# A two-layer graph network on one core: both layer norms of a node computed early, the residual product in a loop of its own

## The chip, the cores and the metric

The kernel runs on one core of a Trainium2 chip. The metric is the time of one execution on the device, in microseconds (us). Three runs of the kernel before took 3151.96, 3153.39 and 3156.57 us, median 3153.39.

## The reference

6250 nodes with 256 features (x), 100,000 edges (src, dst). Every step is added to x:

```python
x = x + _L0_gnn_ref(_layernorm(x), W1, W2, b, src, dst)            # layer 0, graph
x = x + _L0_ffn_ref(_layernorm(x)[None], wr, br, w1, b1, w2, b2)   # layer 0, top-k ffn
x = x + _L1_gnn_ref(_layernorm(x), edges, W, att_src, att_dst, bias, W_res, ...)
x = x + _L1_ffn_ref(_layernorm(x)[None], Wr, br, W1, ..., Wo, bo)  # 8 experts
...
# _L0_ffn_ref
weights = x @ wr + br
sel_idx = top_k(weights, k)[:kk]          # half of the nodes
y = (gelu(x[sel_idx] @ w1 + b1) @ w2 + b2) * weights[sel_idx]
return zeros.at[sel_idx].set(y) + x
...
# _L1_gnn_ref
xn = layer_norm(x, ln1_g, ln1_b)
h = xn @ W                                # 8 heads of 32
e = leaky_relu(a_src[src] + a_dst[dst])   # a_src, a_dst from h
alpha = softmax of e over the edges of each dst (self loops added)
out = segment_sum(h[src] * alpha, dst) + xn @ W_res + bias
out = layer_norm(out, ln2_g, ln2_b)
return out + gelu_tanh(out @ ffn_w1 + ffn_b1) @ ffn_w2 + ffn_b2
```

So layer 1 needs, for each node, x after the layer 0 ffn, and that one depends on whether the node is among the selected half: X + wts * Y for a selected node and X for another, with Y the ffn's output.

## The kernel before

X stays in SBUF as 50 tiles of 125 nodes (NT = 50, NP = 125, D = 256, KD = 2 halves of 128 features). The stages, in order:

- **Start** (to about 165 us of the span). Edges are placed in 17 slots of 128 per tile (SL), layer 0's rows are normalized and stored to gtab in DRAM.
- **First pass** (to 1200). For each tile, POOL gathers 16 to 17 blocks of 128 rows of gtab (L209), TensorE sums them into the tile's nodes with one-hot matrices (L454), and layer 0's graph step follows. `weave` (L1207) strings the tiles' edges (L439) together with the ffn of earlier tiles, in chunks of four tiles (CHUNKS0; the last are of 3, 2 and 1). `weigh0` (L487) normalizes X for the ffn: statistics and root on DVE, z on ACT (L500), X + z written back to X, the selection weight wts on DVE, transposes of z (L506). `ffn0` (L510) is the ffn for all nodes; its output y is stored to ytab in DRAM. The framework's planner orders the engines here: it takes work by its costs and readiness, and may start later code early.
- **Select** (1200–1236). `select` finds the mask of the chosen half, a chain on DVE; wm = wts * mask (L636). The ffn of the last two chunks is traced after it.
- **Nodes' loop of layer 1** (1236–1358). Y is loaded from ytab in ten sets of five tiles, in turn on SP's and ACT's queue (L652). `mix` (L661) works on spans of 1, 2, 2 and then 5 tiles: X += wm * Y (L666), bn_stats and aggregate, one root for the span (`rs`, L182–188). `front` (L673): z on ACT (L676), two transposes (L680), two gains on ACT (L682). Then per tile the product with W and the attention columns, ph (L704, 272 wide), and the one with W_res, pr (L706, 256 wide); ACT evicts h to ht (L707), DVE the attention columns to ASAD (L708) and pr + bias to rr (L709). h goes to htab, rr to rtab. The extremes of the source terms are kept per span. The planner orders all of it.
- **Extremes and branch** (1358–1368). The extremes are reduced over the partitions (L725–733); f1I (L739) says whether the general softmax is needed; all engines load it (L751) and branch (L752). With these inputs the branch isn't taken.
- **Second pass** (1368 to the end). DVE makes the terms adsh of the destinations (L762–770). Per tile there are three groups of six blocks (s counts groups; NG = 3, GS = 6, the last block of a tile being its own rows). `fetch(s)` gathers the rows of htab on POOL into one of four ring buffers and loads own rows on SP; `fetch_tile` loads the one-hot source rows ohT (L812) and rr on SP, `onehot_t` (L819) turns them into one-hot matrices on DVE; `spread` (L827) multiplies them with adsh. Scores, exponentials, sums (L902), layer 1's ffn and the experts follow, woven. Order on PE, DVE and ACT is written by hand (`manual_schedule`, L780), that of POOL and SP is the planner's. POOL also adds the layer's constant to X (`add_o`, L967–969); the planner had 13 of the L968 operations run in the nodes' loop.

Before the second pass starts its rhythm it fetches group 0, the tile's one-hot rows and groups 1 and 2.

Of the kernel before, what the change touches and what calls it, by code (L numbers as in the profile page):

```python
# [18 lines left out]
P = 128  # L19
# [41 lines left out]
def gnn_ffn(ctx, tc, A, out):  # L61
# [114 lines left out]
    def rs(pool, dst, src, mul, add, op0=ALU.mult, name="rs"):  # L176

        p, n = src.shape[0], src.shape[-1]
        v = pool.tile([p, n], F32, name=name + "v")
        y = pool.tile([p, n], F32, name=name + "y")  # L180
        h = pool.tile([p, n], F32, name=name + "h")
# [19 lines left out]
    wm = stat.tile([NP, NT], F32, name="wm")  # L201
    sdT = edge.tile([P, 2, NT, SL], I32, name="sdT")
# [213 lines left out]
    with ExitStack() as p1:  # L416
        wp = p1.enter_context(tc.tile_pool(name="w1", bufs=1))
# [5 lines left out]
        f_w1 = load_w(wp, A["L0_ffn_w1"], "f_w1")  # L423
        f_w2 = load_w(wp, A["L0_ffn_w2"], "f_w2")
        f_b2 = bcast_load(wp, A["L0_ffn_b2"], D, "f_b2")
        f_b1 = load_cols(wp, psum, A["L0_ffn_b1"], "f_b1")
        wrs = bcast_load(wp, A["L0_ffn_wr"], D, "wrs")
        f_br = bcast_load(wp, A["L0_ffn_br"], 1, "f_br")
# [58 lines left out]
        def weigh0(t0, c):  # L487

            xT = pool.tile([P, KD, CT * NP], F32, name="xT")
            made[t0] = xT  # L490
            for j in range(c):
                t = t0 + j
                mv = pool.tile([NP, 2], F32, name="mv")
                bn(pool, mv, X[:, t, :])
                r1 = pool.tile([NP, 3], F32, name="r1")
                rs(pool, r1[:, 0:1], mv[:, 1:2], 1.0, 1e-5)
                nc.vector.scalar_tensor_tensor(r1[:, 1:2], mv[:, 0:1], -1.0, r1[:, 0:1], op0=ALU.mult, op1=ALU.mult)
                nc.vector.tensor_scalar_add(r1[:, 2:3], r1[:, 0:1], 1.0)
                z = pool.tile([NP, D], F32, name="z")
                nc.scalar.activation(z, X[:, t, :], AF.Identity, bias=r1[:, 1:2], scale=r1[:, 0:1])  # L500
                nc.scalar.activation(X[:, t, :], X[:, t, :], AF.Identity, bias=r1[:, 1:2], scale=r1[:, 2:3])
                jk = pool.tile([NP, D], BF16, name="jk2")
                nc.vector.scalar_tensor_tensor(jk, z, 1.0, f_wr, op0=ALU.mult, op1=ALU.mult, accum_out=wts[:, t:t + 1])
                pt = psum.tile([P, KD, NP], F32, name="mi")
# [3 lines left out]
                yield  # L508

        def ffn0(t0, c):  # L510
# [3 lines left out]
            for f in range(NF):  # L514
# [3 lines left out]
                h = pool.tile([P, CT * NP], F32, name="hT", bufs=NF + 1)  # L518
# [3 lines left out]
            for j in range(c):  # L522
                y = pool.tile([NP, 1, D], F32, name="y")
# [4 lines left out]
                ndma(y, ytab, t0 + j, False)  # L528
                yield


        ready = p1.enter_context(ExitStack())
        tmp = ready.enter_context(tc.tile_pool(name="ready", bufs=1))
        far = tmp.tile([1, NT, HEADS], BF16, name="far")
# [29 lines left out]
        def prepare():  # L564
            nc.gpsimd.memset(adsh, 0.0)
            nc.gpsimd.memset(far, FAR)
# [59 lines left out]
        for _ in firsts[-1][1][0]:  # L626
            pass
        for _ in weigh0(*CHUNKS0[-1]):
            pass
        nc.vector.tensor_scalar(wts, wts, f_br[0:NP, :], None, op0=ALU.add)  # L630


        ready.close()
# [993 lines left out]
```

## Time and profile before

| | us |
|---|---|
| median of 3 runs | 3153.39 (3151.96 to 3156.57) |
| the profiled execution | 3153.0 |
| its span | 3151.2 |
| PE, DVE, ACT, POOL busy | 2782.3 (88%), 2019.5 (64%), 1197.9 (38%), 1967.4 (62%) |
| L209 gathers, first pass | 800, mean 0.949 |
| L209 gathers, second pass | 850, mean 1.199 |
| mean granted TensorE clock | 0.946 |

PE is TensorE's matmuls, PEld its weight loads, DVE VectorE, ACT ScalarE, POOL GpSimd, SP the engine that only issues DMAs. Times are from the start of the span. The time of a run is 1.8 us more than the span of the profiled execution. "[5.40 <-DVEq L752]" behind an instruction says that its engine was idle 5.40 us before it, and what it waited for. Busy time of an instruction overlaps that of the next on the same engine, so that starts show the rate better than durations.

### The profile page before, as it was taken

The page shows a single profiled execution, that of the slowest core. Times are in us where ns is not written, and L with a number is a line of the kernel's source. Part 1 is how long each engine was busy: PE and PEld are TensorE (multiplying, and loading weights), DVE is VectorE, ACT ScalarE, POOL GpSimd, SP SyncE. Part 2 cuts the span into 40 slices and gives each one's busy share as a digit, 9 for nine tenths or more (in the row PEclk, how much of TensorE's full clock was granted, in tenths as well). Part 3 has the DMA queues.
Part 4 walks back from the last instruction along what each step waited for, and adds up shares of the span by engine and source line. Part 5 has one row for each costly group of instructions (what it writes and reads, how often), then busy time and mean ns, then how long its engine had stood idle before and what let it go on. Part 6 is the DMA issues. An engine that isn't in the chain of part 4 may idle for free.

```text
span 3151.2 us, 40450 instructions
## 1 busy us (share of the span) xinstructions
PE 2782.3 (88%) x12748; PEld 1979.3 (63%) x12748; DVE 2019.5 (64%) x5683; ACT 1197.9 (38%) x2215; POOL 1967.4 (62%) x1752
## 2 busy tenths in 40 slices
PE   4358889888898896947899999999999999999999
PEld 4345666666666675736776666666666666666665
DVE  7734444444444447857888787777777778787731
ACT  3302222122222222625455455354554545445332
POOL 4677777777777760257777666666666666666400
PEclk8779999999999997968999999999999999999999
DMA  5443343333333335356655545555455454544412
GB/s 124 101 149 103 111 115 112 112 112 111 112 112 112 112 103 127 103 156 177 185 163 148 168 128 149 145 140 157 129 157 146 136 160 126 162 139 137 127 50 60
DMA packets 262780, 407.55 MB, mean 129 GB/s; under 512 B 55283, under 2 KB 202207, under 8 KB 262514
## 3 DMA queue, kind: packets, MB, share of 16 engines
q0 software_dynamic: 80000, 221.18, 25.7%
q1 hardware_dynamic: 169466, 170.78, 18.4%
q10 hardware_dynamic: 13080, 12.80, 1.6%
q8 instruction: 106, 1.74, 0.2%
q14 instruction: 128, 1.05, 0.1%
HBM read 371.33 MB, written 34.04 MB: 129 GB/s over the span
## 4 chain that ended last, share of the span: by engine, by line
PE 45%; DVE 6%; ACT 3%; issue 1%; DMA 1%; POOL 0%; DVEq 0%; ACTq 0%; POOLq 0%
PE ph L1073 19%; PE py L1091 9%; PE iotaP L902 5%; PE py L986 5%; PE ph L975 4%; DVE hrow L892 1%; PE mi L948 1%; DVE lo L882 1%; PE mi L1013 1%; DMA hrow<-htab,sdT 1%; ACT L977 1%; PE pa L827 1%; DVE oh L914 1%; ACT hi L912 1%; ACT hT L977 0%
## 5 line engine op out<-in xcount | busy, mean ns | idle before, releaser
L209 POOL DMA_INDIRECT hrow<-htab,sdT x850 | 1019.3, 1199 | 501.0 <-issue 212.9
L209 POOL DMA_INDIRECT rows<-gtab,sdT x800 | 759.3, 949 | 243.6 <-issue 133.3
L1074 ACT ACTIVATE h<-ph,bi,sc 128x500 f32<-128x500 f32 (+3 forms) x448 | 321.4, 722 | 537.9 <-PE ph L1073 537.6
L454 PE MATMUL ps<-rows,oh 128*125 128x257 f32 x1600 | 434.1, 416 | 60.6 <-DMA rows<-gtab,sdT 50.3
L454 PEld LDWEIGHTS ps<-rows,oh 128*125 128x125 f32 x1600 | 313.7, 204 | 173.5 <-DMA rows<-gtab,sdT 78.5
L1073 PE MATMUL ph<-h,W 128*128 128x500 f32 (+3 forms) x896 | 371.8, 548 | 0.0
L1091 PE MATMUL py<-Wo,h 128*125 128x256 f32 x1600 | 369.3, 380 | 0.4 <-ACT h L1074 0.4
L1073 PE MATMUL ph<-wcat,W 128*128 128x500 f32 (+3 forms) x896 | 365.6, 547 | 2.3 <-ACT h L1074 2.2
L1091 PEld LDWEIGHTS py<-Wo,h 128*125 128x125 f32 x1600 | 296.3, 188 | 71.8 <-issue 28.3
L892 DVE TENSOR_TENSOR hrow<-hrow 128x768 f32<-128x768 f32 x300 | 280.5, 975 | 73.8 <-ACT hrow L877 73.8
L1094 DVE SCALAR_TENSOR_TENSOR X<-py,gate,X 125x256 f32<-125x256 f32 x400 | 173.5, 478 | 202.8 <-PE py L1091 202.6
L882 DVE SCALAR_TENSOR_TENSOR lo<-hrow,hi 128x792 fp32r<-128x792 f32 (+1 forms) x300 | 287.0, 998 | 0.0
L912 ACT ACTIVATE hi<-hrow 128x792 fp32r<-128x792 f32 (+1 forms) x300 | 236.8, 823 | 124.5 <-DVE hrow L892 124.3
L902 PE MATMUL iotaP<-hi,oh 128*125 128x264 f32 x850 | 252.2, 329 | 0.0
L1073 PEld LDWEIGHTS ph<-wcat,W 128*128 128x128 f32 x896 | 162.4, 194 | 140.9 <-issue 109.8
L1073 PEld LDWEIGHTS ph<-h,W 128*128 128x128 f32 x896 | 159.6, 194 | 106.3 <-issue 95.8
L902 PE MATMUL iotaP<-lo,oh 128*125 128x264 f32 x850 | 219.9, 291 | 4.8 <-DVE lo L882 4.7
L517 PE MATMUL ph<-xT,f_w 128*128 128x500 f32 (+3 forms) x448 | 190.2, 550 | 0.5 <-ACT xT L507 0.5
L975 PE MATMUL ph<-xT,h_w 128*128 128x500 f32 (+3 forms) x448 | 185.1, 554 | 5.1 <-ACT hT L977 4.0
L526 PE MATMUL py<-f_w,hT 128*125 128x256 f32 x800 | 182.8, 381 | 1.2 <-DVE y L527 0.4
L986 PE MATMUL py<-h_w,hT 128*125 128x256 f32 x800 | 177.6, 380 | 0.0
L902 PEld LDWEIGHTS iotaP<-lo,oh 128*125 128x125 f32 x850 | 162.7, 191 | 20.6 <-issue 8.3
(331 smaller groups left out, 3874.5 us busy)
## 6 DMA issues: line engine op xcount, KB each, us to landing
W<-in_L_ffn_W SPq DMA_DIRECT2D x224, 256.0 KB
Wo<-in_L_ffn_Wo SPq DMA_DIRECT2D x112, 256.0 KB
ohT<-dltab SPq DMA_DIRECT2D x50, 535.5 KB
hrow<-htab,sdT POOLq DMA_INDIRECT x850, 3.3
rows<-gtab,sdT POOLq DMA_INDIRECT x800, 2.8
hrow<-htab SPq DMA_DIRECT2D x50, 115.5 KB
X<-in_x ACTq DMA_DIRECT2D x10, 560.0 KB
ytab<-y SPq DMA_DIRECT2D x50, 112.0 KB
```

Source lines behind the costliest of these rows:

```text
L209: nc.gpsimd.indirect_dma_start(out=dst, out_offset=None, in_=tab, in_offset=bass.IndirectOffsetOnAxis(ap=idx, axis=0))
L454: nc.tensor.matmul(ps, oh[:, i, :], edge_rows[i], start=(s0 + i == 0), stop=(s0 + i == SL - 1))
L517: nc.tensor.matmul(ph[:, 0:n], f_w1[:, k, f * P:(f + 1) * P], xT[:, k, 0:n], start=(k == 0), stop=(k == KD - 1))
L882: nc.vector.scalar_tensor_tensor(L["lo"][:, c], L["rows"][:, c], 1.0, L["hi"][:, c].bitcast(F32), op0=ALU.mult, op1=ALU.subtract)
L892: nc.vector.tensor_tensor(h4, h4, rows[:, c, D:, None].to_broadcast([P, GS // 2, HEADS, HD]), ALU.mult)
L902: nc.tensor.matmul(tiles[t]["ps"], L["oh"][:, i, :], r[:, i, :], start=(g + i + q == 0), stop=(g * GS + i == SL - 1 and q == 1))
L912: nc.scalar.activation(L["hi"][:, c], L["rows"][:, c], AF.Copy)
L975: nc.tensor.matmul(ph[:, 0:n], h_w1[:, k, f * P:(f + 1) * P], C["xT"][:, k, 0:n], start=(k == 0), stop=(k == KD - 1))
L986: nc.tensor.matmul(py[:, i, :], C["hT"][f][:, j * NP:(j + 1) * NP], h_w2[:, f, :], start=(f == 0), stop=(f == NF - 1))
L1073: nc.tensor.matmul(ph[:, 0:n], w[:, k, f * P:(f + 1) * P], rhs[:, k, 0:n], start=(k == 0), stop=(k == KD - 1))
L1074: nc.scalar.activation(h[:, f, 0:n], ph[:, 0:n], AF.Relu, bias=cols[1][:, f, e:e + 1], scale=cols[0][:, f, e:e + 1])
L1091: nc.tensor.matmul(py[:, i, :], hidden[u, "2"][:, k, j * NP:(j + 1) * NP], weights[u, "Wo"][:, k, :], start=(k == 0), stop=(k == KD - 1))
```

## The change

For each node both layer norm statistics, that of X and that of X + wts * Y, are made in the first pass, before the mask is known; after the select the mask chooses between them. `weigh0` derives the first from those it has; `ffn0` forms x2 = y * wts + X and takes its statistics. Roots are taken per chunk (`roots_of`), once more for the last two chunks. The nodes' loop then has only mix, z, transposes, gains and the product with W, in an order written by hand for PE, DVE, ACT and POOL (`steps`: the number is how many tiles a step is ahead of the product). Its z is on DVE for each third tile, one of the two gains is on DVE, ACT evicts all 272 columns. The transposed inputs are kept where Y was, and a second loop multiplies them with W_res, two tiles per eviction, with the terms of the destinations in between. The edges of the first four groups and the first one-hot rows are fetched ahead of it and of the branch; the branch's arm makes terms and one-hot anew. Y's tiles lie on the right side of SBUF and are all loaded on SP's queue; the pools of the ffn's tiles are apart from those of the edges. In the second pass most groups are fetched one group further ahead, in quarter 2.

```diff
@@ in the first pass
+        late = p1.enter_context(tc.tile_pool(name="late", bufs=2))
+        lw = p1.enter_context(tc.tile_pool(name="latew", bufs=1))
...
             for j in range(c):
                 t = t0 + j
...
                 nc.vector.scalar_tensor_tensor(jk, z, 1.0, f_wr, op0=ALU.mult, op1=ALU.mult, accum_out=wts[:, t:t + 1])
+                nc.vector.tensor_copy(mv2[:, 0, t, 0:1], mv[:, 0:1])
+                nc.vector.scalar_tensor_tensor(mv2[:, 0, t, 1:2], mv[:, 1:2], r1[:, 2:3], r1[:, 2:3], op0=ALU.mult, op1=ALU.mult)
...
+            nc.vector.tensor_scalar(wts[:, t0:t0 + c], wts[:, t0:t0 + c], f_br[0:NP, :], None, op0=ALU.add)
+
+        def roots_of(a, b, name):
+
+            rs(late, r2[:, :, 0, a:b], mv2[:, :, a:b, 1], 1.0 + 1e-5, 1e-10, name=name)
+            nc.vector.scalar_tensor_tensor(r2[:, :, 1, a:b], mv2[:, :, a:b, 0], -1.0, r2[:, :, 0, a:b], op0=ALU.mult, op1=ALU.mult)
...
                 ndma(y, ytab, t0 + j, False)
+                t = t0 + j
+                x2 = late.tile([NP, D], F32, name="x2", bufs=1)
+                nc.vector.scalar_tensor_tensor(x2, y[:, 0, :], wts[:, t:t + 1], X[:, t, :], op0=ALU.mult, op1=ALU.add)
+                bn(late, mv2[:, 1, t, :], x2)
                 yield
+            if t0 < CHUNKS0[-2][0]:
+                roots_of(t0, t0 + c, "ra")
...
@@ select
-        nc.vector.tensor_scalar(wts, wts, f_br[0:NP, :], None, op0=ALU.add)
-        sl = p1.enter_context(tc.tile_pool(name="sl", bufs=1))
+        sl = p1.enter_context(tc.tile_pool(name="sl", bufs=1, side="right"))
         mask = select(tc, sl, psum, wts, ident, iota, ones, upto)
         nc.vector.tensor_tensor(wm, wts, mask, ALU.mult)
+        other = sl.tile([NP, NT], F32, name="other")
+        nc.vector.tensor_scalar(other, mask, -1.0, 1.0, op0=ALU.mult, op1=ALU.add)
...
+            nc.vector.tensor_tensor(part[:, :, a:b], r2[:, 1, :, a:b], mask[:, None, a:b].to_broadcast(sh), ALU.mult)
+            nc.vector.tensor_tensor(r2[:, 0, :, a:b], r2[:, 0, :, a:b], other[:, None, a:b].to_broadcast(sh), ALU.mult)
+            nc.vector.tensor_tensor(r2[:, 0, :, a:b], r2[:, 0, :, a:b], part[:, :, a:b], ALU.add)
+
+        take(0, CHUNKS0[-2][0])
         for t0, c in CHUNKS0[-2:]:
             for _ in ffn0(t0, c):
                 pass
+        roots_of(CHUNKS0[-2][0], NT, "rb")
+        take(CHUNKS0[-2][0], NT)
...
@@ the nodes' loop
+        wp = mid.enter_context(tc.tile_pool(name="mw", bufs=1, side="right", reuse_waits="tile"))
...
-            ndma(Y[-1], ytab, t0, True, eng=(nc.sync, nc.scalar)[(t0 // XC) % 2])
+                ndma(y, ytab, t0, True)
...
-        spans = [(0, 1), (1, 2), (3, 2)] + [(t, MC) for t in range(5, NT, MC)]
+        mid.enter_context(tc.manual_schedule(engines={mybir.EngineType.PE, mybir.EngineType.DVE, mybir.EngineType.Activation, mybir.EngineType.Pool}))
+        groups = [(t, 5) for t in range(0, 45, 5)] + [(45, 3), (48, 2)]
+        xTs = [Y[t // XC][:, t % XC, 0:KD * NP].rearrange("p (k m) -> p k m", k=KD) for t in range(NT)]
...
+            if t % 3 == 2:
+                nc.vector.tensor_scalar(zs[t], X[:, t, :], r, m, op0=ALU.mult, op1=ALU.add)
+            else:
+                nc.scalar.activation(zs[t], X[:, t, :], AF.Identity, bias=m, scale=r)
...
+            nc.scalar.activation(xTs[t][:, 0, :], pt[:, 0, :], AF.Identity, bias=ln1_b[:, 0:1], scale=ln1_g[:, 0:1])
+            nc.vector.tensor_scalar(xTs[t][:, 1, :], pt[:, 1, :], ln1_g[:, 1:2], ln1_b[:, 1:2], op0=ALU.mult, op1=ALU.add)
...
+            nc.scalar.activation(ht[:, t - t0, :], phs.pop(t), AF.Copy)
+            if t == t0 + c - 1:
+                ndma(ht[:, 0:c, 0:HW], htab, t0, False)
+                nc.vector.tensor_copy(ASAD[:, t0:t + 1, :], ht[:, 0:c, D:HA])
+                if t + 1 in (20, 40, 48, NT):
+                    greatest({20: 0, 40: 20, 48: 40, NT: 48}[t + 1], t + 1)
+
+        steps = ((8, lambda t: nc.vector.scalar_tensor_tensor(X[:, t, :], Y[t // XC][0:NP, t % XC, :], wm[:, t:t + 1], X[:, t, :],
+                                                              op0=ALU.mult, op1=ALU.add)),
+                 (0, product), (3, turn), (-1, evict), (2, gain), (5, norm))
+        for i in range(-8, NT + 1):
+            for lead, f in steps:
+                if 0 <= i + lead < NT:
+                    f(i + lead)
+
+        for k in range(len(ring)):
+            fetch_edges(k)
+        nc.vector.tensor_scalar(ext[:, HEADS:], ext[:, HEADS:], -1.0, None, op0=ALU.mult)
+        first_onehot()
...
@@ after the extremes
+        made_terms = terms_by_parts()
+        for t in range(0, NT, 2):
+            pr = psum.tile([NP, 2, D], F32, name="pr")
+            for i in range(2):
+                for k in range(KD):
+                    nc.tensor.matmul(pr[:, i, :], xTs[t + i][:, k, :], wcat[:, k, HA:HA + D], start=(k == 0), stop=(k == KD - 1))
...
+            nc.vector.tensor_tensor(rr[:, j:j + 2, :], pr, g_bias[0:NP, None, :].to_broadcast([NP, 2, D]), ALU.add)
+            if j == 2 or t + 2 == NT:
+                ndma(rr[:, 0:j + 2, :], rtab, t - j, False)
+            if t >= 10:
+                next(made_terms, None)
...
         mid.close()
         gen1 = nc.values_load(f1I[0:1, 0:1], min_val=0, max_val=1)
         with tc.If(gen1 > 0):
...
+            terms()
+            first_onehot()
...
@@ the second pass
-            if s >= 1:
+            if s >= 2 and (s - 1) % NG == 0:
                 fetch(s + len(ring) - 2)
...
         def quarter2(s):
 
+            if s >= 1 and s % NG != 0:
+                fetch(s + len(ring) - 1)
...
+        fetch_tile(0)
+        for k in range(len(ring)):
+            own_rows(k)
         load(0, ("W1", "W2", "Wo"))
         load(1, ("W1", "W2"))
-        fetch(0)
-        fetch_tile(0)
-        for k in range(1, len(ring) - 1):
-            fetch(k)
-        onehot_t(0)
         spread(0)
```

## The prediction

> **What bounds the kernel now.** I first cut the span into stages and read the busy time of each engine in every stage. The columns are the stretch, its length, then busy us (and instructions) of PE, PEld, DVE, ACT and POOL, the granted TensorE clock, the DMA share and GB/s.
>
> ```profile
> core 0: us, PE busy (x) PEld busy (x) DVE busy (x) ACT busy (x) POOL busy (x), PEclk, DMA share, GB/s
> 200.00:1200.00 1000.00, 883.96 (x3524) 651.89 (x3522) 443.69 (x1982) 222.04 (x447) 734.96 (x773) 0.94 0.38 108
> 1200.00:1236.00 36.00, 16.78 (x90) 14.35 (x89) 27.32 (x84) 3.61 (x10) 0.16 (x1) 0.73 0.68 165
> 1236.00:1247.00 11.00, 1.15 (x5) 0.71 (x5) 10.80 (x59) 1.73 (x4) 1.66 (x5) 0.50 1.08 235
> 1247.00:1310.00 63.00, 56.11 (x262) 44.87 (x262) 63.00 (x301) 42.53 (x107) 15.06 (x7) 0.97 0.34 99
> 1310.00:1358.00 48.00, 47.09 (x234) 39.19 (x234) 23.25 (x93) 35.34 (x91) 14.23 (x6) 1.00 0.42 124
> 1370.00:1389.00 19.00, 0.01 (x1) 0.01 (x1) 4.71 (x10) 0.00 (x0) 14.32 (x14) 0.50 0.79 208
> 1389.00:1413.00 24.00, 11.11 (x64) 9.22 (x64) 21.26 (x39) 8.83 (x13) 19.12 (x17) 0.50 0.52 145
> 1640.00:3151.00 1511.00, 1491.87 (x6617) 989.75 (x6615) 1102.39 (x2402) 706.08 (x1102) 883.78 (x708) 1.00 0.48 135
> ```
>
> Four regimes are to be seen. In the first pass (to 1200) POOL looks only 73% busy, but a gather takes 0.95 us plus 0.30 of issue: one every 1.25, and a chunk's 65 gathers make 81.2 us, which is the measured period of a chunk. POOL paces it. Then the select runs on DVE (1200–1236), TensorE idles until the first product (1247), and the nodes' loop runs to 1358 with TensorE 89 to 98% busy. From 1358 to 1389 TensorE does nothing: the branch and the start of the second pass. From 1640 the second pass is TensorE-bound (98.7%): what the diff does there can only shift it as a whole. So the change is worth what it moves between 1170 and about 1450, minus any harm in the first pass.
>
> The waits of TensorE inside the first pass come second, as they tell how much of it is slack (us in total, times, longest):
>
> ```profile
> PE mi L506 <- ACT z L500: 59.3, 12, 5.5
> PE ps L454 <- DMA rows<-gtab,sdT: 46.6, 74, 6.5
> ```
>
> Once per chunk TensorE waits some 5 us for the LN output z, and afterwards it waits again for gathered rows: 46.6 / 12 = 3.9 us per chunk is what a longer first wait may eat for nothing.
>
> Third, the timeline, for one tile of the loop in its later half, and for the start of the second pass (start, us, engine, line, idle before and releaser):
>
> ```profile
> 1340.77 0.38 PE L680 MATMUL mi<-ident,z 125*128 125x125 f32 x2
> 1340.99 1.08 PE L704 MATMUL ph<-wcat,xT 128*125 128x272 f32 x4
> 1341.91 1.03 PE L706 MATMUL pr<-wcat,xT 128*125 128x256 f32 x4
> 1342.77 0.38 PE L680 MATMUL mi<-ident,z 125*128 125x125 f32 x2
> ```
>
> From starts: transposes 0.22, ph 0.92, pr (W_res) 0.86, together 2.00 per tile.
>
> ```profile
> 1367.84 0.64 DVE L764 TENSOR_TENSOR shift<-shift,ASAD 125x24 f32<-125x24 f32 x2 [5.40 <-DVEq L752]
> 1370.72 1.14 POOL L209 DMA_INDIRECT hrow<-htab,sdT  x1 [15.82 <-DVE rem L770]
> 1388.15 0.79 DVE L819 TENSOR_SCALAR ohT<-ohT,pcol 126x2176 bf16<-126x2176 bf16 x1 [14.22 <-DMA ohT<-dltab]
> 1388.99 0.42 PE L827 MATMUL pa<-adsh,ohT 126*128 126x48 bf16 x6 [27.88 <-DMA hrow<-htab,sdT]
> ```
>
> The branch costs DVE 5.40; TensorE's first spread at 1388.99 follows the one-hot rows, whose load stood behind other loads on SP's queue; the first gather goes at 1370.72.
>
> **The change, part by part.** The reference point is the first spread at 1388.99.
>
> *First pass.* Per tile it adds two [125,1] operations (0.15 each), x2 (125x256, 0.48 as L482, of the same shape), bn_stats 0.42 and bn_aggr 0.18: 1.38 us; per chunk 13 small root operations at 0.17, 2.2. That is 4 x 1.38 + 2.2 = 7.7 per chunk on DVE, which is 36.4 of 81 busy: 44.1 still fits beneath POOL's 81.2. What can cost is order, the new work standing ahead of the z chain on DVE: 0.5 to 1 us per chunk, covered by the 3.9. If that cover were gone it would cost 12 us per us. I take 0 for the chunks and +1 (0 to 3) after the last gather.
>
> Here a rule speaks against x2. The row: between 200 and 1170 the spacing of 790 gathers exceeds 1.25 by 4.9 us in total although 50 L482 operations with two SBUF inputs run beside them, so 50 more cost at most some 5. The Trainium skill, "SBUF — State Buffer", section "Who interferes with whom", says that a DVE instruction with two SBUF inputs contends with a GpSimd instruction that reads SBUF; if each x2 held up a gather for its length, 50 x 0.48 = 24 us would be added and the forecast would be 3151. The same section infers that such an operation takes only the read interface, which descriptor generation doesn't need; the row agrees, so the sum goes by the row.
>
> *Select.* wts + bias moves out (−0.16). Added on DVE: x2 and statistics of the last four tiles (about 1.1 each, partly in the 8.7 us that DVE is idle in 1200–1236), 13 root operations and 7 of choosing at 0.17. Bounds +1 (all in idle time but the choosing) to +6 (half of all); I take +3.5. The mask-dependent weights, ready at 1235.4, thus come at 1239.9.
>
> *Start of the nodes' loop.* Before, mix at 1236.2, first statistics, roots on a DVE busy 10.80 of 11, z at 1244.4, product at 1247.0. Now no statistics: mix 0.5, z 0.6, transposes 0.4, gain 0.45, product, with handovers 2.6. Y's tiles are loaded into other memory; at 1236–1247 the DMA share was 1.08, and one tile set of 640 KB at that stretch's 235 GB/s is 2.7 us. If the first one must wait for the select's own tiles it costs up to 6; if not, 0. No row tells which memory it takes; I take +2.5. First product at 1239.9 + 2.6 + 2.5 = 1245.0.
>
> *Loop 1.* TensorE per tile 2.00 − 0.86 = 1.14, so 57 us for 50. ACT per step: z on two of three tiles (0.593), one gain (0.452), one eviction (0.384): 1.23 if nothing overlaps, 0.97 by the spacing of back-to-back ones (0.49, 0.345, 0.30). DVE: mix 0.40, half the gains 0.2, a third of z 0.14, little else: 0.75. The old first half ran with DVE at 63.00 of 63; the statistics leave, so that bound leaves. I add 2 for a cold clock and 6 (0 to 15) for engines handing on within a step that is only 1.14 long: 65 us, to 1310. POOL's additions L968 ran 13 times in the old loop, 2.25 each, and a DVE mix beside one took 1.92 instead of 0.5; hoisted there or not, that lies inside the 0 to 15.
>
> *Extremes, then W_res.* The chain from the last product to the shift took 1358.3–1362: 4 us, TensorE idle, then 50 x 0.86 = 43 us and 1.5 for the clock. I read that from 584.42, where 24 matmuls after a wait of 5.20 took 7.35 instead of 2 x 2.77. End at 1310 + 4 + 44.5 = 1358.5. rr (25 of 0.68, as the 125x512 eviction from PSUM) and the 14 terms (about 9) make 26 of DVE's 43: hidden. The 23 gathers of the first four groups at 1.25 to 1.5 take 29 to 35 from about 1312, done by 1347: hidden. The store of four-tile rr sets goes behind SP's other work and no one waits but tile 0's.
>
> *Branch.* Register load 0.85 and branch 5.04 on TensorE: +6, so 1364.5; the one-hot rows and terms are already there, a spread follows at about 1365: −24. If the one-hot load still sat behind the branch it would be −20.
>
> *Rows ahead.* Before, gather 24 was issued 13.9 after the first spread (1402.88); now it can be about 9 after: at most −5. A loss is not excluded, since own rows, loads and the one-hot rows change places on SP's queue, where L812 stood behind 4 us of other issues: up to +4. POOL idled 5.45 at 1445 for free buffers, so most of the lead is lost there: −2.
>
> Sum: −24 − 2 = −26; 3151.2 − 26 = 3125.2, with the 1.8 around the span **3127**. The profiled execution took 3153.0 against a median of 3153.39, so nothing is added for that.
>
> **The rivals.**
> - *The first pass becomes late.* For: TensorE's longest recurrent wait is for DVE's chain by way of z, and the new x2 has one buffer, so that DVE, filled in bursts at the chunk's end, may delay it. Against: DVE at 54% after, 3.9 us of slack per chunk. Price: 12 x (d − 3.9) for a delay d per chunk. At d = 6.1 the whole 26 is gone; at 7, 3164. This is the case on the other side.
> - *Loop 1 is set by handing on, not by TensorE.* A step of 1.6 (ACT's 1.23 and three waits of some 0.12, as between the chained operations of the old extremes chain) makes 80 + 2 where I have 65: +17, 3144. From 1.78 on nothing is gained. Against: four tiles of lead, and no buffer is reused in the very next step.
> - *Rows ahead don't help.* DVE bounds the first 24 us of the second pass in any case (21.26 of 24 busy), and SP's new order costs its 4: the rest shifts by 24 − 4 = 20: 3133.
> - *More is gained.* No jitter (6), Y in time (2.5), the bound of select (2.5) and of rows ahead (3): 26 + 14 = 40: 3113.
>
> **How the numbers follow.** My own case, 3116–3140, has 0.60, of it 0.15 for rows ahead that don't help; more gained 0.08; loop 1 by handing on 0.14 (3140–3152, of it 0.03 no longer faster); the first pass late 0.11, of it 0.09 slower by over 0.2%, some 6.3 us, about what a measurement of this kernel can tell from no change; 0.07 for what I don't see, 0.03 faster, 0.02 same, 0.02 slower. Faster 0.60 + 0.08 + 0.11 + 0.03 = 0.82, same 0.03 + 0.02 + 0.02 = 0.07, slower 0.11. The range for 8 in 10 goes from 3106 (the low bounds of select, Y, jitter, rows ahead and the tail together) to 3148 (a step of about 1.7): above it lie the late first pass, a part of the third case and some of the unseen, 0.18; below it 0.02.
>
> **What would show it.** Right: chunks of the first pass still 81 us; the mixes of loop 1 spaced 1.1 to 1.3; an unbroken W_res stretch of 43; 23 gathers ahead of the branch; first spread near 1365; the stretch from 1640 merely shifted. Wrong: the wait for z beyond 9 us per chunk with rows no longer waited for; mixes spaced above 1.6; first mix later than 1246; a first spread that again waits for one-hot rows.

## The result and the profile after

The changed kernel takes 3137.85 us (median of five runs, 3137.0 to 3141.61); the kernel before, five times on the same chip, 3153.55. The ratio is 0.995, with a 95% interval of 0.9936 to 0.9965: 15.7 us are gained. 26 were forecast; the direction was right, and 3137.85 lies in the stated range of 3106 to 3148. The profiled execution took 3140.49, its span 3138.7.

First the same stretches of the changed kernel as were shown of the one before (length, then busy us and instructions of PE, PEld, DVE, ACT and POOL, granted TensorE clock, DMA share, GB/s):

```profile
core 0: us, PE busy (x) PEld busy (x) DVE busy (x) ACT busy (x) POOL busy (x), PEclk, DMA share, GB/s
200.00:1200.00 1000.00, 874.03 (x3481) 643.47 (x3481) 506.43 (x2347) 217.46 (x437) 733.84 (x773) 0.94 0.38 108
1200.00:1236.00 36.00, 23.43 (x122) 19.66 (x120) 29.32 (x116) 7.62 (x19) 1.09 (x4) 0.84 0.12 41
1247.00:1310.00 63.00, 56.15 (x259) 42.59 (x260) 57.15 (x118) 46.35 (x118) 27.24 (x13) 0.88 0.60 157
1310.00:1358.00 48.00, 43.58 (x196) 36.24 (x196) 28.21 (x68) 7.89 (x18) 26.21 (x25) 0.96 0.64 183
1370.00:1389.00 19.00, 4.34 (x30) 3.54 (x30) 11.23 (x22) 4.18 (x7) 5.76 (x6) 0.62 0.69 184
1389.00:1413.00 24.00, 12.90 (x67) 11.08 (x68) 19.53 (x44) 9.99 (x16) 19.45 (x18) 0.57 0.56 151
1640.00:3138.00 1498.00, 1479.66 (x6558) 980.85 (x6556) 1091.62 (x2381) 699.53 (x1092) 874.17 (x699) 1.00 0.48 135
```

DVE has 63 us more to do in the first pass (506.43 for 443.69), and POOL does the same work in the same time (733.84 for 734.96): the gathers weren't slowed. TensorE is at 98.8% from 1640, as before. Everything happens in between. In 1200–1236 TensorE does 23.43 where it did 16.78: the layer 0 ffn runs later. In the loop DVE is again 91% busy. The next table puts the stages side by side; its times are read from the timelines of the two profiled executions: starts, but for the products and W_res, which go to the end of their last matmul.

| us | before | after |
|---|---|---|
| last gather of the first pass | 1168.8 | 1167.9 |
| from there to the start of the selection chain | 32.0 | 41.7 |
| from there to the mask-dependent weights | 34.7 | 36.2 |
| from there to the first product | 11.6 | 4.7 |
| products (before: with W_res) | 111.7 | 71.8 |
| extremes | 4 | 3.0 |
| W_res | in the products | 44.1 |
| first spread (its time) | 1388.99 | 1374.53 |
| from the first spread to the first transpose of a finished tile (`o`) | 27.8 | 29.4 |
| from there to the end of the span | 1734.4 | 1734.8 |

The first spread comes 14.5 earlier, the stage behind it takes 1.6 more and the rest 0.4 more: together the 12.5 by which the spans differ.

The waits of TensorE in 200–1190 (us in total, times, longest):

```profile
PE mi L509 <- ACT z L501: 59.7, 13, 6.8
PE ps L455 <- DMA rows<-gtab,sdT: 45.6, 80, 6.3
```

Up to 1170 they are 55.3 in 12 waits for z and 45.6 for rows, to be set against 59.3 and 46.6 before; the thirteenth wait for z, 4.31, falls behind the last gather. Within the chunks little has changed: the cover held. The start of the second pass, in the timeline (start, us, idle before and releaser):

```profile
1374.53 0.38 PE L909 MATMUL pa<-adsh,ohT 126*128 126x48 bf16 x6 [5.01 <-DVEq L867]
1389.51 0.42 PE L909 MATMUL pa<-adsh,ohT 126*128 126x48 bf16 x6 [5.22 <-DVE ohT L901]
```

TensorE stood idle for 27.88 before its first spread and waits 5.01 now, for the branch and nothing else. The second line is the spread of the next tile: its one-hot rows come late, and it waits 5.22 where it waited 2.58 before. That takes back 2.6 of what the stage after the spread should have gained.

### The profile page after: what moved, and what is told of

Same layout as the page of the kernel before. It is cut to its first block, busy times and chain, and to the rows that moved or that the text cites. A ratio compares the mean times of both kernels' runs of the same rounds, so it can differ in the third digit from the quotient of the medians.

```text
span 3138.7 us, 40435 instructions
## 1 busy us (share of the span) xinstructions
PE 2786.7 (89%) x12748; PEld 1981.1 (63%) x12748; DVE 2081.0 (66%) x5836; ACT 1170.0 (37%) x2149; POOL 1964.4 (63%) x1752
## 4 chain that ended last, share of the span: by engine, by line
PE 47%; DVE 6%; ACT 1%; issue 1%; DMA 1%; POOL 0%; DVEq 0%; SPq 0%; ACTq 0%; POOLq 0%
PE ph L1157 19%; PE py L1175 9%; PE iotaP L986 5%; PE py L1070 5%; PE ph L1059 5%; DVE hrow L976 1%; PE mi L1032 1%; PE mi L1097 1%; DMA hrow<-htab,sdT 1%; DVE lo L964 1%; PE pa L909 1%; DVE oh L998 0%; DVE bnst L190 0%; POOL hrow L208 0%; ACT hi L996 0%
```

## The experiments

All times are medians, with the ratio to the kernel before on the same chip and its 95% interval. The short diffs are against the changed kernel; against the kernel before only where that is said. "Tail" stands for the time from the last gather to the selection chain.

### What the second statistics cost

One kernel leaves out the second layer norm's statistics (x2, its bn_stats and its roots); the weights r2 are set to one, so the output isn't the reference's.

```diff
+    nc.gpsimd.memset(r2, 1.0)
...
-                x2 = late.tile([NP, D], F32, name="x2", bufs=1)
-                nc.vector.scalar_tensor_tensor(x2, y[:, 0, :], wts[:, t:t + 1], X[:, t, :], op0=ALU.mult, op1=ALU.add)
-                bn(late, mv2[:, 1, t, :], x2)
...
-                roots_of(t0, t0 + c, "ra")
...
-        roots_of(CHUNKS0[-2][0], NT, "rb")
```

> Leaves out x2, its statistics and all roots of r2 in the first pass (r2 is set to 1 instead), so the nodes' second layer norm is not computed; all else as in the changed kernel (3137.85 us). Theory: the new DVE work is free while gathers pace the pass, and costs only after the last gather, where it reorders DVE: the selection begins 41.7 us after the last gather in the changed kernel and 32.0 before the change; without the statistics it should be back at 32 to 33, the selection should be 1 to 2 us shorter, and the time 3126 to 3129. Rival 1: the statistics hold up gathers all along (24 us by the length of x2): the last gather then comes 10 to 24 us earlier than 1167.9 and the time is 3105 to 3118. Rival 2: the late start of the selection comes from the other edits of the first pass (split pools, mv2): the selection still begins 41 us after the last gather, time 3135 to 3138.

Measured 3112.6 us (0.9867, 0.9851 to 0.9884), 25 less than the changed kernel. The last gather is at 1167.5, so the 50 x2 operations hold up no gather. The tail is 23.3: 18.4 shorter than after the change, and 8.7 shorter than before it. Of the rest, 6.2 are in loop 1 (65.7 instead of 71.8) and 1.9 in the select. And the wait for z is gone from the first pass; the time is spent waiting for rows:

```profile
PE ps L456 <- DMA rows<-gtab,sdT: 90.3, 157, 6.4
PE mi L510 <- ACT z L502: 1.2, 1, 1.2
```

The two timelines of TensorE at the end of the first pass show what this is worth once there are no rows left to wait for. First the changed kernel, then the one without second statistics:

```profile
1180.86 2.33 PE L455 MATMUL ps<-rows,oh 128*125 128x257 f32 x10
1187.51 1.26 PE L509 MATMUL mi<-ident,z 125*128 125x125 f32 x4 [4.31 <-ACT z L501]
1188.97 6.94 PE L455 MATMUL ps<-rows,oh 128*125 128x257 f32 x20 [0.19 <-DVE oh L452]
```

```profile
1168.72 2.33 PE L456 MATMUL ps<-rows,oh 128*125 128x257 f32 x10
1170.90 0.38 PE L510 MATMUL mi<-ident,z 125*128 125x125 f32 x2
1171.11 2.77 PE L456 MATMUL ps<-rows,oh 128*125 128x257 f32 x12
```

The last twenty matmuls on gathered rows start at 1188.97 in the one and at 1171.11 in the other, with the last gather issued at 1167.9 and 1167.5. TensorE works in order: a late z makes the ffn of its chunk late, so that TensorE is still at an older ffn until 1180.9 in the changed kernel, and then it stands before the transposes of the next z for 4.31, with the sums queued behind. Some of the delay comes from before the last gather: the ten matmuls of the first line start 12.98 behind it, in the kernel before 7.96 (1176.76), so that 5.0 of the 9.7 by which the tail has grown are there already.

Why is z late? DVE isn't busy. In one chunk of the changed kernel, DVE's timeline has X of three tiles finished at 522.85, 537.44 and 556.22, but the first bn_stats of an X (`bnst<-X`) at 576.93, behind the last of the four of an x2 (`bnst<-x`). Each x2 waits for TensorE's product py, and DVE is idle for 7.5 us in between:

```profile
556.22 0.48 DVE L483 SCALAR_TENSOR_TENSOR X<-e,inv,X 125x256 f32<-125x256 f32 x1
...
565.74 0.42 DVE L536 TENSOR_TENSOR y<-py,f_b 125x256 f32<-125x256 f32 x1 [7.51 <-PE py L535]
...
576.58 0.43 DVE L190 BATCH_NORM_STATS2 bnst<-x 125x6 f32<-125x256 f32 x1
576.93 0.41 DVE L190 BATCH_NORM_STATS2 bnst<-X 125x6 f32<-125x256 f32 x1
```

Without the second statistics it follows X within 0.7 us:

```profile
554.39 0.49 DVE L484 SCALAR_TENSOR_TENSOR X<-e,inv,X 125x256 f32<-125x256 f32 x1
...
555.12 0.42 DVE L190 BATCH_NORM_STATS2 bnst<-X 125x6 f32<-125x256 f32 x1
```

Both uses of `bn` take their small tile `bnst` from one ring of two buffers, in the pool `late`. This is the rule in the first pass: from 200 to 1210, the statistics of X start more than 5 us behind X in 34 of the 49 tiles whose statistics the trace has, by up to 57.5; in the kernel before in none (at most 1.25), without the second statistics in none (at most 4.0). Whether this ring sets it is taken up below.

### Is it the roots, or the last tiles' statistics?

Two versions shorten the tail's own DVE work. One puts the roots of chunk 44–46 with the last ones; one also takes that chunk's x2 and statistics out of the tail, from y read back from ytab after the select (`second` is x2 and its bn; `ffn0` calls it for the other chunks only).

```diff
-            if t0 < CHUNKS0[-2][0]:
+            if t0 < CHUNKS0[-3][0]:
                 roots_of(t0, t0 + c, "ra")
...
-        take(0, CHUNKS0[-2][0])
+        take(0, CHUNKS0[-3][0])
...
-        roots_of(CHUNKS0[-2][0], NT, "rb")
-        take(CHUNKS0[-2][0], NT)
+        roots_of(CHUNKS0[-3][0], NT, "rb")
+        take(CHUNKS0[-3][0], NT)
```

```diff
+        t0, c = CHUNKS0[-3]
+        yb = sl.tile([NP, c, D], F32, name="yb")
+        ndma(yb, ytab, t0, True)
+        for j in range(c):
+            second(t0 + j, yb[:, j, :])
```

> Moves only the 13 root operations of the chunk of three tiles (44 to 46) from the end of the first pass to the roots taken after the selection has begun. Theory A, these roots standing among those of tiles 47 and 48 make z late: interleaved operations cost some 13 x 0.07 = 0.9 us directly, so at most 1 to 2 us of the 9.8 come back, time 3136 to 3137. Theory B, the planner's whole order hangs on them: the selection begins 32 to 34 us after the last gather, time 3128 to 3131.

> x2, its statistics and the roots of the chunk of three tiles (44 to 46) are made beside the selection, from y loaded back from ytab. Theory: with no second statistics between the last gather and the selection, the chain of tiles 47 and 48 stands where it stood before the change, z comes 4 us earlier, TensorE keeps its clock, and the selection begins 32 to 34 us after the last gather; the selection itself grows by 1 to 3 us: time 3129 to 3133. Rival: the order is spoilt by the smaller operations of weigh0 (mv2) or by the pools: selection still at 40 or more after the last gather, time 3138 to 3141.

Roots late: 3135.44 us (0.9936, 0.992 to 0.9953), tail 41.2. The roots aren't it. Chunk 44–46 late as well: 3132.52 (0.9932, 0.9916 to 0.9949), tail 37.0. That is 4.7 of the 9.7 that the tail has grown by, and the lowest median of the complete versions; its interval overlaps those of the changed kernel, of the roots late and of the third ht buffer below, so that no order among them is shown. The wait behind the last gather is gone; the twelve within the chunks remain, 55.1 in total (55.3 after the change). TensorE comes to the same ten matmuls on rows at 1179.93, 0.9 earlier than in the changed kernel. What is left of the tail's growth is thus mostly the delay that it brings from the chunks before.

### POOL's additions in the loop

In the changed kernel all 14 of POOL's additions of the constant to X (L1052) run in loop 1. One version adds the constant to o, in the second pass; one keeps the additions ahead of the second pass, but only five (AHEAD) in the loop over the steps and nine behind the 23 gathers.

```diff
-            nc.gpsimd.tensor_tensor(X[:, t0:t0 + n, :], X[:, t0:t0 + n, :], cst[0:NP, None, :].to_broadcast(bc), ALU.add)
+            nc.gpsimd.tensor_tensor(o[:, 0:n, :], o[:, 0:n, :], cst[0:NP, None, :].to_broadcast(bc), ALU.add)
```

```diff
+        def add_cst(ci):
+            t0, n = CHUNKS1[ci]
+            nc.gpsimd.tensor_tensor(X[:, t0:t0 + n, :], X[:, t0:t0 + n, :], cst[0:NP, None, :].to_broadcast([NP, n, D]), ALU.add)
...
+            if i >= 4 and (i - 4) % 9 == 0 and (i - 4) // 9 < AHEAD:
+                add_cst((i - 4) // 9)
...
+        for ci in range(AHEAD, len(CHUNKS1)):
+            add_cst(ci)
...
-            nc.gpsimd.tensor_tensor(X[:, t0:t0 + n, :], X[:, t0:t0 + n, :], cst[0:NP, None, :].to_broadcast(bc), ALU.add)
```

> POOL adds the constant of the layer to the layer's output instead of to X, the same number of POOL operations, but none of them can run before the second pass. Theory: in loop 1 a mix beside a POOL addition takes 2.26 us instead of 0.47; 14 of those are 25 us of DVE, of which DVE's slack of 0.3 us per step hides about 15; without them the mixes' mean falls from 0.80 to 0.47 and loop 1 (71.8 us from first to last product) is 4 to 8 us shorter: 3130 to 3134 if the second pass bears the 14 additions for nothing. Rival: loop 1 waits for TensorE and for the htab store only, so that it stays at 70 to 72, and the additions then press on the second pass: 3138 to 3145.

> POOL's additions of the layer's constant to X are put by hand: five in loop 1, nine behind the 23 gathers, beside the W_res loop; none in the second pass. Theory: loop 1 loses nine of its 14 DVE stalls of 1.8 us: 62 to 66 instead of 71.8; beside W_res the additions cost nothing (DVE reads PSUM there), and the second pass is as in the changed kernel, not 20 us longer as with all additions in it: 3128 to 3133. Rival: the additions hold up the POOL's branch, so that the second pass starts as late as before: 3136 to 3140.

With the constant added to o, loop 1 takes 61.3 us instead of 71.8. The groups of the mix (shape, count, busy us, mean ns of one, idle before) in the stretch 1225–1325 say why, first the changed kernel, then this one:

```profile
L784 DVE SCALAR_TENSOR_TENSOR X<-Y,wm,X 125x256 f32<-125x256 f32 x50 | 39.5, 798 | 0.0
```

```profile
L784 DVE SCALAR_TENSOR_TENSOR X<-Y,wm,X 125x256 f32<-125x256 f32 x50 | 23.4, 475 | 0.0
```

And one pair in the timeline of the changed kernel:

```profile
1297.73 0.47 DVE L784 SCALAR_TENSOR_TENSOR X<-Y,wm,X 125x256 f32<-125x256 f32 x1
...
1298.76 2.38 POOL L1052 TENSOR_TENSOR X<-X,cst 125x1024 f32<-125x1024 f32 x1 [2.72 <-ACT z L744]
1299.15 2.26 DVE L784 SCALAR_TENSOR_TENSOR X<-Y,wm,X 125x256 f32<-125x256 f32 x1
```

A mix that starts beside one of POOL's additions ends 0.27 after it: 2.26 instead of 0.47. This takes 16 us of a DVE that has 57 of 63 to do. But the whole took 3152.69 us (0.9994, 0.9984 to 1.0003): the gain is given back, and more. From the first transpose of o to the end it takes 1756.1 instead of 1734.8, and TensorE has a wait in 1640–3000 that the changed kernel doesn't have:

```profile
PE pa L909 <- DVE ohT L901: 13.9, 9, 1.6
```

That is 13.9 of the 21; no wait is named here for the other 7. In both versions POOL does the constant's work, and of the two places the loop was the cheaper.

With five in the loop, the profiled execution did what was expected: loop 1 65.0, second pass 1734.2, 3131.9 us. But ten more runs took 3149.18 to 3157.45; the median of all eleven is 3150.88 (0.9994, 0.9985 to 1.0004). The profile is that of the first; where the others spend 20 us more isn't seen. This stays open, and the version can't be called a gain.

### The two loops, and the rows ahead

One version puts the product with W_res back into the first loop, with rr evicted tile by tile and the terms made behind it; the second loop is removed. The other keeps both loops, but fetches the edges of the first four groups only behind the branch.

```diff
+            prs[t] = psum.tile([NP, D], F32, name="pr")
+            for k in range(KD):
+                nc.tensor.matmul(prs[t], xTs[t][:, k, :], wcat[:, k, HA:HA + D], start=(k == 0), stop=(k == KD - 1))
...
+            nc.vector.tensor_tensor(rrs[t0][:, t - t0, :], prs.pop(t), g_bias[0:NP, :], ALU.add)
...
```

```diff
-        for k in range(len(ring)):
-            fetch_edges(k)
         nc.vector.tensor_scalar(ext[:, HEADS:], ext[:, HEADS:], -1.0, None, op0=ALU.mult)
...
         for k in range(len(ring)):
+            fetch_edges(k)
             own_rows(k)
```

> Puts the product with W_res back into the loop of the product with W (rr evicted tile by tile on DVE, stored with h); terms, first one-hot rows and the gathers of four groups stay in front of the branch, but now nothing of TensorE's lies above them. Theory: the split itself costs TensorE 3.0 us (the extremes) and a cold clock, and buys the cover for 23 gathers (29 us), 14 terms (9 us) and the one-hot rows. In one loop TensorE takes 50 x 2.00 = 100 us and some 5 of stalls from 1250.5, ends near 1356, the terms go on DVE to 1368, the branch takes 5, first spread 1373 to 1376 as before, but the gathers begin only after the last store, near 1357, so that the first group is there at 1368 and group 4 some 25 us later: 3140 to 3148. Rival: rows and terms are hidden anyway and the split is worth nothing or costs: 3132 to 3138.

> The gathers of the first four groups go behind the branch again; one-hot rows, terms and W_res loop as in the changed kernel. Theory: first spread at 1374.5 as with the rows ahead, but the first scores wait for six gathers (some 10 us with the descriptor start of 1.7) and the first two tiles go at the pace of the gathers: 12 to 20 us later, 3150 to 3158. Rival (mine of the prediction: rows ahead don't help since DVE bounds the start): 3138 to 3143.

One loop: 3149.86 us (0.9987, 0.9978 to 0.9997). The first spread comes at 1366.8, earlier than in the changed kernel (1374.5), and still the kernel is 12 us slower. Its gathers can start only with the loop's last store, at 1354.79, and the last of the 23 is issued at 1383.70. ACT then waits long for rows; in the timeline:

```profile
1354.79 0.97 POOL L208 DMA_INDIRECT hrow<-htab,sdT  x1 [10.78 <-DMA htab<-ht]
...
1393.27 1.62 ACT L988 ACTIVATE hi<-hrow 128x792 fp32r<-128x792 f32 x2 [22.13 <-DMA hrow<-htab,sdT]
```

It isn't the first rows that ACT waits for: DVE had read the first group's at 1370.17 and the second's at 1374.25. ACT's instruction waits for many transfers at once, and the profile puts it down to a gather; which one it is stays open.

Rows not ahead: 3152.98 us (0.9998, 0.9988 to 1.0008). The first spread is at 1371.3, also earlier than in the changed kernel. The gathers start at 1372.67, as late as before the change (1370.72), and the second pass is as late as before too: the first transpose of o is at 1415.9 (1416.8 before). Its timeline:

```profile
1372.67 0.97 POOL L208 DMA_INDIRECT hrow<-htab,sdT  x1 [57.24 <-DVE ad L939]
...
1388.29 0.21 DVE L941 TENSOR_TENSOR w<-hrow,ad 128x48 f32<-128x48 f32 x1 [15.98 <-DMA hrow<-htab,sdT]
```

So the start of the second pass is not set by the first spread. Without rows ahead it is set by the arrival of the first rows; in one loop by a later transfer, a gather by the profile. The second loop is worth 12 us and the rows ahead 15. That they are nearly the same gain, with the W_res stretch as the cover under which the rows are fetched, fits the first transposes of o (at 1415.1 in one loop and 1415.9 without rows ahead); no version shows it apart.

### The store that stands behind the loads of Y

The FFN weights of layer 1 are loaded on SP ahead of Y; moved behind loop 1 in the program text, and with a third ht buffer:

```diff
-        h_w1 = load_w(w2, A["L1_gnn_ffn_w1"], "h_w1")
-        h_w2 = load_w(w2, A["L1_gnn_ffn_w2"], "h_w2")
...
-                hts[t0] = pool.tile([NP, 5, HA], F32, name="ht")
+                hts[t0] = pool.tile([NP, 5, HA], F32, name="ht", bufs=3)
...
+        h_w1 = load_w(w2, A["L1_gnn_ffn_w1"], "h_w1")
+        h_w2 = load_w(w2, A["L1_gnn_ffn_w2"], "h_w2")
         for k in range(len(ring)):
```

> The loads of layer 1's ffn weights are traced after loop 1 instead of before it, and ht has three buffers instead of two. Theory: in the changed kernel the load of those weights waited on SP for the last roots (6.8 us), all Y behind it, and the first htab store behind all Y, so that ACT waited 4.55 us for a ht buffer and TensorE 3.24 and ran at half clock after it. Without it no such wait: loop 1 at 64 to 67 instead of 71.8, time 3131 to 3134. Rival: the planner's noise in the wait is what moves loop 1 (68.1 in the two runs that changed the first pass alone): 68 to 70, 3135 to 3137.

Measured 3135.78 us (0.9943, 0.9927 to 0.996); against the changed kernel 2 less, which the intervals don't separate. The planner issued the weights ahead of Y all the same, so only the third buffer had an effect. In the changed kernel's timeline the first eviction to reuse a buffer waits for the first group's store. That had its turn on SP (SPq is its queue) at 1262.85 only, behind 22 loads of Y that began at 1233.19:

```profile
1233.19 27.82 SPq L85 DMA_DIRECT2D Y<-ytab  x22
1262.85 3.24 SPq L87 DMA_DIRECT2D htab<-ht  x4
...
1269.94 0.40 ACT L777 ACTIVATE ht<-ph 125x272 f32<-125x272 f32 x1 [4.55 <-DMA htab<-ht]
1270.39 2.18 PE L760 MATMUL ph<-wcat,Y 128*125 128x272 f32 x4 [3.24 <-ACT ht L777]
```

With three buffers this wait is gone and loop 1 takes 65.4. The kernel without second statistics agrees: it has two buffers, but ACT waits only 0.8 for such a store, and its loop 1 takes 65.7. The last line shows what such a pause costs beyond itself: the four matmuls behind it take 2.18, where the same four take 1.08 at 1318.30 (the granted clock is 0.57 in 1268–1276 and 0.95 in 1316–1322).

### The shared ring by itself

In four more runs x2's statistics have a ring of their own (alone; with the edit of the store; that pair once more), and the kernel before gets its own rings for `weigh0`, as there the edges and the ffn share them.

```diff
-                bn(late, mv2[:, 1, t, :], x2)
+                st2 = late.tile([NP, 6], F32, name="bnst2")
+                nc.vector.bn_stats(st2, x2)
+                nc.vector.bn_aggr(mv2[:, 1, t, :], st2)
```

and in the kernel before:

```diff
-                bn(pool, mv, X[:, t, :])
+                stw = pool.tile([NP, 6], F32, name="bnstw")
+                nc.vector.bn_stats(stw, X[:, t, :])
+                nc.vector.bn_aggr(mv, stw)
...
-                rs(pool, r1[:, 0:1], mv[:, 1:2], 1.0, 1e-5)
+                rs(pool, r1[:, 0:1], mv[:, 1:2], 1.0, 1e-5, name="rw")
```

> In the changed kernel x2's statistics and those of weigh0 take their small bn_stats result from the same ring of two buffers (bnst, 24 bytes each). Here x2's gets a ring of its own; the work is the same to the last instruction. Theory: what made z late in the first pass was no engine but this ring: weigh0's statistics had to wait until those of x2, which wait for TensorE, had given a buffer back. With its own ring z comes early, TensorE's 59.7 us of waits for z become waits for gathered rows, the selection begins 23 to 26 us after the last gather instead of 41.7, and the time is 3119 to 3124. Rival: it is the DVE time of x2 itself (1.1 us per tile) that fills the chunk's end: selection at 38 to 42, time 3135 to 3139.

> The own ring of e9 together with the later loads of the ffn weights and the third ht buffer of e7. Theory: the two act in different stages and add up: selection 23 to 26 us after the last gather, loop 1 at 65 us, 2 to 3 us less than with the ring alone: 3116 to 3121. Rival: Y's loads, asked for 16 us earlier, are in time anyway, and the second edit is worth nothing more: within 1 us of the ring alone.

> The kernel before the change, with nothing but names: the statistics and roots of weigh0 take their buffers from rings of their own instead of those that the graph step's roots use. Theory: the wait for z of 59.3 us in the first pass goes, the selection begins 23 to 25 us after the last gather instead of 32.0, and the time falls by 7 to 9 us, to 3144 to 3147: that much of the changed kernel's potential has nothing to do with its statistics or loops. Rival: the late z of the kernel before had another cause, selection still at 32: 3152 to 3155.

> The kernel of e10 once more, since the three runs before it went to a chip on which the kernel before the change itself took 3597 us, with TensorE waiting for its own instructions in the first pass. It differs from e7 (3135.78 us, selection 41.4 us after the last gather) by the ring of x2's bn_stats alone. Theory: weigh0's statistics waited for that ring; with a ring of its own the selection begins 23 to 26 us after the last gather, TensorE's waits for z of about 59 us in the first pass become waits for gathered rows, and the time is 3116 to 3121. Rival: the DVE time of x2 is what delays z: selection at 38 to 42, 3134 to 3138.

These four ran on two other chips, on which the kernel before itself takes 3596.87 and 3552.18 us. The first three came to 3598.56, 3602.17 and 3608.89 (ratios 1.0001, 1.0006 and 1.0029, the last with 1.0003 to 1.0055), the fourth to 3566.42 (1.0025, 0.9993 to 1.0057). The order came out as the theory has it: with the own ring the statistics of X start more than 5 us behind X in none of 50 tiles (at most 2.2; in the two versions with the other edit 2.7 and 2.1). In the kernel before it is the roots that the shared ring holds up, more than 5 us behind the statistics in 35 tiles; with own rings in none (at most 1.6). DVE's timeline with the own ring, with the statistics of X right behind X and those of x2 (L542) after them, in the version with this edit alone:

```profile
608.02 0.48 DVE L483 SCALAR_TENSOR_TENSOR X<-e,inv,X 125x256 f32<-125x256 f32 x1
...
608.76 0.42 DVE L190 BATCH_NORM_STATS2 bnst<-X 125x6 f32<-125x256 f32 x1
...
609.59 0.43 DVE L542 BATCH_NORM_STATS2 bnst<-x 125x6 f32<-125x256 f32 x1
```

What it is worth can't be read there, as TensorE and not POOL paces the first pass on these chips. In that version it ends at 1588.7 instead of 1168, TensorE waits hardly at all for z or rows (in all four, at most 3.0 for z and 3.6 for rows), and it stands still without a cause that the profile shows ("issue"):

```profile
PE mi L468 <- issue: 159.4, 21, 32.1
PE mi L474 <- ACT uT L470: 95.7, 26, 9.1
```

As the edit changes only the ring, and the order on DVE is set before the program runs, the ring is shown as the cause of the order, and the tail's lost time is shown to come from the second statistics; that it comes by way of the ring is argued, and how many of the 18 us the own ring brings back where POOL paces the pass is open. So is whether it adds up with the late chunk 44–46.

## Why the prediction was right, and where it was wrong

*The chunks of the first pass, taken at 0: right.* The last gather is 0.9 earlier; DVE's 62.7 us more are 5.2 per chunk, for 7.7 reckoned. The Trainium skill, "SBUF — State Buffer", section "Who interferes with whom", says that a DVE instruction with two SBUF inputs contends with a GpSimd instruction that reads SBUF; it infers, for `tensor_tensor`, that such an operation takes only the read interface while descriptor generation needs the write interface. The traces agree in that the gathers aren't held up (the last at 1167.9 with 50 x2 operations, 1167.5 without); which interface either uses they don't show. For a plain addition on POOL the same rule shows in full: 2.26 against 0.47.

*After the last gather, +1 (0 to 3): wrong, +9.7.* This is the term that was mis-sized most, 8.7 of the 11 to 13.5 that are missing. The prediction saw that order, not DVE's load, was what could cost, and let the wait for rows cover it. It didn't ask where that cover ends: at the end of the pass no rows are waited for, and a late z is paid in full. It also took the wait for z as given; it comes from the order of work on DVE and can be made to go, as the 1.2 without second statistics (59.3 before) shows. This is the rival of the late first pass, in the one place where it had no slack. In the chunks the rival is refuted: the gathers didn't become later.

*The select, +3.5 (1 to 6): +1.5.* Hardly any of the last tiles' statistics lengthens the select itself; what they cost is in the term above. *First product, 5.1 behind the weights: 4.7*, with Y in time.

*Loop 1, 65: 71.8 in this profile, 68.1 to 68.3 in three other profiles that have the same loop, and 65.7 in the one without second statistics.* What differs among these five goes with the wait for the ht store: 5.3 in all, 2.6 to 3.3, and 0.8. The 6 us for handing on were too few by 1 to 7. It wasn't handing on: without POOL's additions it is 61.3, with a third ht buffer 65.4. The prediction had the row (a mix of 1.92 beside an addition) and left it inside a range instead of multiplying it: 13 additions by 1.4 would have been 18, and the mixes' excess is 16.1 (39.5 against 23.4). The rival of a 1.6 us step is refuted in its mechanism; of its price of 17 came 6.8.

*Extremes, W_res and branch, 4, 44.5 and 6: 3.0, 44.1 and 5.0.* Right, and so was the half-clock allowance. First spread at 1374.5 instead of about 1365.

*Rows ahead, −2 (−5 to +4): +1.6 by the profile, but 15 by the experiment.* Of the term as written, how far ahead the later groups run, nothing came: the one-hot rows of the second tile hold up the spread for 5.22. But the division of the gain was wrong. All 24 were credited to the earlier spread and 2 to the rows; the versions that lack one of the two, the second loop or the rows, reach a spread at 1366.8 or 1371.3 and end within 4.3 us of the kernel before. The sum came out near because both are in the changed kernel. That 3137.85 still lies in the prediction's own case, 3116 to 3140, is partly luck: the tail and loop 1 alone were 15.5 too short, others 6.1 too long, and the profiled execution, 3140.49, lies just outside. The rival that rows ahead don't help is refuted.

*From 1640: unchanged*, as said. *More is gained* did not happen; the late chunk 44–46 brings 5.3 of it.

Taken together: +8.7 for the tail, −2.4 for the select and the start, +6.8 for loop 1, −2.8 from the end of loop 1 to the first spread, −0.9 for an earlier last gather and +4.0 behind the spread give 13.4, where 13.5 lie between the predicted span of 3125.2 and that of the profiled execution; the median of the runs is 2.6 below that execution.

## What to carry to other kernels

Where slack covers a delay in every round of a pipeline, look at the last round by itself: there is no next round to catch up in, and the delay is paid in full. When an in-order engine waits though the one it waits for is idle, look for a small buffer ring that two uses share; it can order them without either being busy. And to start a stage earlier, find what it waits for last (here transfers, the gathered rows above all, not the product that was so visibly late) and put the work that doesn't need it on top of that wait.

## What the runs showed of the hardware that wasn't expected

- A DVE operation with two SBUF inputs that met a POOL addition ran until that addition ended, and 0.27 more: 2.26 us instead of 0.47, with 125x1024 on POOL. Beside POOL's gathers the same form costs the gathers nothing (1167.9 and 1167.5).
- After an idle stretch the matmuls of one line took twice as long (2.18 for four against 1.08, at a granted clock of 0.57 and 0.95), so that a wait of 3.2 in loop 1 costs more than 3.2.
- The same kernel before takes 3153, 3552 or 3597 us on different chips. On the two slower chips it wasn't profiled itself; in the four profiles of versions taken there the granted clock is 0.99 to 1.00 in 2000–3000 too, but 0.81 in 200–1580, for 0.94 in 200–1200 here. The first pass is what is longer (it ended at 1586 to 1600 in these four profiles, for 1168), and in the one shown above over 200 us of it are waits of TensorE that the profile explains by nothing.
- One version gave 3131.9 us once and 3149 to 3157 in ten other runs on one chip. A single run, and a single profile, could have been taken for a gain of 20 us.
